# A GRU step with its gates reordered, its sigmoid halves folded into the blend, and its last channel block worked by batch element

## The chip, the cores and the metric

The kernel runs on one core of a Trainium2 chip. The metric is the device time of one execution in microseconds (us), the median over several executions. All runs compared here are of the undisturbed ("fast") state. The engines are called PE (matmuls), DVE (vector), ACT (activations) and POOL (GpSimd), as the profile calls them; the recorded texts also say TensorE, VectorE and ScalarE. An fp32 matmul or transpose of the source appears in the trace as two instructions, and counts below are of those.

## The reference

There are 64 graphs of 256 nodes with 256 channels. The first layer, a gated graph network, is nearly all of the work, and the change is in it:

```python
h = relu(layernorm(x))
for i in range(3):                                    # three steps
    m    = h @ weight[i]
    aggr = einsum('bst,bsd->btd', adj != 0, m)        # sums over neighbours
    gi, gh = aggr @ w_ih.T + b_ih, h @ w_hh.T + b_hh  # split into r, z, n
    r = sigmoid(i_r + h_r);  z = sigmoid(i_z + h_z)
    n = tanh(i_n + r * h_n)
    h = (1 - z) * n + z * h
x = x + h
# second layer: h = relu(layernorm(x)), graph attention with 4 heads, x = x + its output
```

## The kernel before

Two graphs make a pair (512 columns), and there are 32 pairs. A pair is a Python generator that emits its instructions stage by stage, and two pairs are interleaved, so that the attention part of the older pair lies beside the gates of the newer. When the program is built, a scheduler turns all this into one fixed list of instructions for each engine. As its lists show, it keeps roughly to the order of emission, but moves work forward that it takes to be ready.

The weights of the message are folded into those of the gates, so a step is: transpose h to rows and split it into hi and lo (`prows`), sum over neighbours (`pa`), then for each of two channel blocks the gates `hn, r, z, in` and the blend:

```python
for l in range(L):
    if l:
        rows_hi_lo(KD - 1, hT, hi, lo)          # rows of the last channel block (PE, then ACT and DVE)
    for e in range(KD):
        neighbours(e, aggr, hi, lo)             # sums of channel block e, both graphs
        yield                                   # a stage ends at each yield
    for c in range(KD):
        gate(p_hn, wT["hh"], g_n, hT, True, True)
        gate(p_r, wT["hh"], g_r, hT, True, False);  gate(p_r, w_in[:, l], g_r, aggr, False, True)
        gate(p_z, wT["hh"], g_z, hT, True, False);  gate(p_z, w_in[:, l], g_z, aggr, False, True)
        gate(p_in, w_in[:, l], g_n, aggr, True, True)
        # r = 0.5*tanh(./2)+0.5 (ACT, DVE); z likewise (ACT, POOL)
        # t = (p_hn + bh) * r; t = p_in + t (DVE); n = tanh(t + bi) (ACT)
        # d = h - n (POOL); d = z * d; hT2 = n + d (DVE)
        if c < KD - 1: yield
    ...                                         # rows of the first channel block of the next step
    yield
# transposes back (pback), x1 = x + h; yield; norm_relu_T(x1): second norm and its transposes (pt_b); yield
# val (pv); yield; attention: prow, softmax, ppT, po ...
STEPS = 1 + L * (2 + KD) + 3 + PB * (1 + KN)     # 22
# a new pair starts every STEPS // 2 + 1 = 12 stages
```

`hT` is the state with channels on the partitions, `aggr` the sums. Some names for later: a row join is the place between two steps where PE needs the rows of the last channel block (`prows`); a pair has two. The half-k matmuls of a gate are those that take the first channel block of h, which is ready a stage earlier. `pt_a` are the transposes after a pair's first norm; `zz`, `lk` and `nmx` belong to the softmax. A bank is one of the PSUM buffers into which PE writes; the program has four for the gates and four for the rest. Filler is work that stands in PE's list ahead of an instruction that waits.

Of the kernel before, what the change touches and what calls it, by code (L numbers as in the profile page):

```python
# [9 lines left out]
F32 = mybir.dt.float32  # L10
# [3 lines left out]
AF = mybir.ActivationFunctionType  # L14
ALU = mybir.AluOpType
AX = mybir.AxisListType

P = 128
# [4 lines left out]
EPS = 1e-5  # L23
# [3 lines left out]
def gated_gnn_then_gat_kernel(  # L27
# [25 lines left out]
    nc = tc.nc  # L53
    B, N, D = x.shape
    L = weight.shape[0]
# [3 lines left out]
    KD = D // P  # L59
# [14 lines left out]
    def bank(name):  # L74
        return ps_m.tile([P, 512], F32, tag="mm", name=name)
# [71 lines left out]

    w_nat = sb.tile([P, KD, D], F32, tag="d", name="w_nat")
# [36 lines left out]
    def norm_relu_T(src, name):  # L185

        st = small.tile([P, R, 6], F32, tag="st", name=f"st_{name}")
        mv = small.tile([P, R, 2], F32, tag="mv", name=f"mv_{name}")
        for r in range(R):
            nc.vector.bn_stats(st[:, r, :], src[:, r, :])  # L190
            nc.vector.bn_aggr(mv[:, r, :], st[:, r, :])
        rstd = small.tile([P, R], F32, tag="rstd", name=f"rstd_{name}")
        nc.vector.tensor_scalar_add(rstd, mv[:, :, 1], EPS)
        nc.gpsimd.tensor_tensor(rstd, rstd, mhalf, ALU.pow)
        xn = sb.tile([P, R, D], F32, tag="xn", name=f"xn_{name}")
        for r in range(R):
            nc.vector.tensor_scalar(
                xn[:, r, :], src[:, r, :], mv[:, r, 0:1], rstd[:, r : r + 1], op0=ALU.subtract, op1=ALU.mult
            )
        hT = sb.tile([P, KD, T], F32, tag="hT", name=f"hT_{name}", bufs=4)  # L200
        for k in range(KD):
            pt = bank(f"pt_{name}_{k}")
            for r in range(R):
                nc.tensor.transpose(pt[:, ts(r, P)], xn[:, r, ts(k, P)], ident)
            nc.scalar.activation(hT[:, k, :], pt, AF.Relu)
        return hT, xn

    def gate(pt, w, g, src, start, stop):
        for k in range(KD):
            nc.tensor.matmul(  # L210
                pt, w[:, k, ts(g, P)], src[:, k, :], start=start and k == 0, stop=stop and k == KD - 1
            )

    def pair(p):
# [6 lines left out]
        hT, xn = norm_relu_T(xt, f"a{p}")  # L221
# [7 lines left out]
        def rows_hi_lo(k, hT, hi, lo):  # L229

            pt = bank(f"prows_{hi.name}_{k}")
            for r in range(R):
                nc.tensor.transpose(pt[:, ts(r, P)], hT[:, k, ts(r, P)], ident)  # L233
            pt = pt.rearrange("q (r d) -> q r d", r=R)
            nc.scalar.copy(hi[:, :, ts(k, P)], pt)
            nc.vector.tensor_sub(lo[:, :, ts(k, P)], pt, hi.bitcast(F32)[:, :, ts(k, P)])

        def neighbours(e, aggr, hi, lo):
            pt = bank(f"pa_{aggr.name}_{e}")
            for i in range(PB):  # L240
                for s in range(KN):
                    for part in (hi, lo):
                        nc.tensor.matmul(  # L243
                            pt[:, ts(i, N)], part[:, i * KN + s, ts(e, P)], edge[:, i * KN + s, :],
                            start=(s == 0 and part is hi), stop=(s == KN - 1 and part is lo),
                        )
            nc.scalar.copy(aggr[:, e, :], pt)

        for l in range(L):
            n_ = f"{p}_{l}"  # L250
            aggr = sb.tile([P, KD, T], F32, tag="aggr", name=f"aggr_{n_}")
            if l:
                rows_hi_lo(KD - 1, hT, hi, lo)
            for e in range(KD):
                neighbours(e, aggr, hi, lo)
                yield
            hT2 = sb.tile([P, KD, T], F32, tag="hT", name=f"hT_{n_}", bufs=4)
            for c in range(KD):
# [7 lines left out]
                gate(p_r, w_in[:, l], g_r, aggr, False, True)  # L266
                gate(p_z, wT["hh"], g_z, hT, True, False)
                gate(p_z, w_in[:, l], g_z, aggr, False, True)
                gate(p_in, w_in[:, l], g_n, aggr, True, True)

                r_ = sb.tile([P, T], F32, tag="r", name=f"r_{n_}_{c}")
                nc.scalar.activation(r_, p_r, AF.Tanh, bias=brz[:, g_r : g_r + 1], scale=0.5)  # L272
                nc.vector.tensor_scalar(r_, r_, 0.5, 0.5, op0=ALU.mult, op1=ALU.add)  # L273
                z_ = sb.tile([P, T], F32, tag="z", name=f"z_{n_}_{c}")
                nc.scalar.activation(z_, p_z, AF.Tanh, bias=brz[:, g_z : g_z + 1], scale=0.5)  # L275
                nc.gpsimd.tensor_scalar(z_, z_, 0.5, 0.5, op0=ALU.mult, op1=ALU.add)  # L276
                t_ = sb.tile([P, T], F32, tag="t", name=f"t_{n_}_{c}")
                nc.vector.scalar_tensor_tensor(
                    t_, p_hn, bh[:, g_n : g_n + 1], r_, op0=ALU.add, op1=ALU.mult
                )  # L280
# [6 lines left out]
                nc.vector.tensor_mul(d_, z_, d_)  # L287
                nc.vector.tensor_add(hT2[:, c, :], n__, d_)  # L288
                if c < KD - 1:
                    yield  # L290
            if l < L - 1:
                if p == 0:
                    fold(l + 1)
                hi = sb.tile([P, R, D], F32R, tag="hi", name=f"hi_{p}_{l + 1}")
                lo = sb.tile([P, R, D], F32R, tag="lo", name=f"lo_{p}_{l + 1}")
                for k in range(KD - 1):
                    rows_hi_lo(k, hT2, hi, lo)
# [17 lines left out]
        hT, _ = norm_relu_T(x1, f"b{p}")  # L315
# [79 lines left out]
    STEPS = 1 + L * (2 + KD) + 3 + PB * (1 + KN)  # L395
# [41 lines left out]
```

## Time and profile before

| | before |
|---|---|
| time | 3027.39 us (3025.45 to 3027.95) |
| PE busy | 2891.5 of 3024.3 us, 96% |
| DVE, ACT, POOL busy | 58%, 32%, 17% |
| start of the first pair's `pback`, of the last pair's, end | 110.23, 2964.27, 3024.3 us |
| one pair in mid run | 92.07 us |

The best tool to find PE's gaps is the timeline of PE alone. Subtract from each distance between two starts what that instruction takes when nothing is in its way (a gate 0.429 us, `po` 0.1115, `pa` 0.1185, `pv` 0.223, a transpose 0.109); what is left over is lost. One stretch that the prediction does not show, in front of `pt_b`, looks like this (start, duration, engine, line, instruction, and in brackets how long PE was idle and for whom):

```profile
1495.30 0.88 PE L307 MATMUL pback<-ident,hT 128*128 128x128 f32 x6 [0.56 <-DVE hT L288]
1496.02 1.88 PE L210 MATMUL pr<-hT_a,hh_T 128*128 128x512 f32 x4
1497.73 1.02 PE L210 MATMUL pr<-aggr,w_in 128*128 128x512 f32 x2
1498.59 1.88 PE L210 MATMUL pz<-hT_a,hh_T 128*128 128x512 f32 x4
1501.17 0.67 PE L204 MATMUL pt_b<-ident,xn_b 128*128 128x128 f32 x4 [0.69 <-DVE xn_b L197]
```

Between the last `pback` and `pt_b` the list of PE holds 10 gate matmuls of the newer pair (10 x 0.429 = 4.29 us). The second norm takes longer than that, and 0.86 us are lost (the bracket says 0.69, because the modelled end of a matmul lies some 0.16 us after its slot).

### The profile page before, as it was taken

The numbers are of one execution on the slowest core, as the hardware profiler recorded it, in microseconds if no ns is written. First come the engines' busy times: TensorE is split into PE (matmuls) and PEld (weight loads), VectorE is DVE, ScalarE is ACT, GpSimd is POOL, SyncE is SP. The second block draws the span as 40 slices with busy tenths as digits, with TensorE's granted clock in tenths as the row PEclk, the third lists the DMA queues.
The fourth block names the chain that finished last, engine by engine and source line by source line (L and its number), as shares of the span: only waits on it lengthen the run. The fifth ranks groups of instructions, "written<-read, shape, count | busy, mean of one in ns | idle before, by whom it ended". The sixth has DMA issues, their size and how long they took to land.

```text
span 3024.3 us, 31009 instructions
## 1 busy us (share of the span) xinstructions
PE 2891.5 (96%) x11620; PEld 1689.6 (56%) x11620; DVE 1753.5 (58%) x3428; ACT 969.2 (32%) x2177; POOL 520.0 (17%) x583
## 2 busy tenths in 40 slices
PE   7999999999999999999999999999999999999996
PEld 4555555555555555555555555555555555555554
DVE  4555665555665555655556655556655566555554
ACT  1223332323333233333233323333332333233332
POOL 1111111111111111111111111111111111111111
PEclk9999999999999999999999999999999999999996
DMA  2000000000000000000000000000000000000000
GB/s 79 8 21 17 19 15 14 22 21 15 22 15 15 21 21 15 14 15 21 22 15 21 15 14 21 22 14 15 18 18 22 15 21 15 15 21 15 7 6 9
DMA packets 56085, 55.07 MB, mean 18 GB/s; under 512 B 4096, under 2 KB 55936, under 8 KB 55936
## 3 DMA queue, kind: packets, MB, share of 16 engines
q1 hardware_dynamic: 50688, 50.34, 5.3%
q10 hardware_dynamic: 5248, 2.76, 0.3%
q8 instruction: 92, 1.51, 0.2%
q14 instruction: 57, 0.47, 0.1%
HBM read 36.32 MB, written 16.78 MB: 18 GB/s over the span
## 4 chain that ended last, share of the span: by engine, by line
PE 71%; DVE 14%; POOL 6%; ACT 4%; issue 4%; DMA 0%; POOLq 0%; SPq 0%; DVEq 0%; ACTq 0%
PE pz L210 16%; PE pr L210 15%; PE pin L210 9%; PE po L382 7%; PE phn L210 7%; PE pa_aggr L243 5%; PE pv L321 4%; POOL d L286 4%; PE ppT L372 3%; DVE d L287 2%; DVE hT L288 2%; ACT pr L363 2%; DVE zz L346 2%; PE prows_hi L233 2%; ACT n L283 2%
## 5 line engine op out<-in xcount | busy, mean ns | idle before, releaser
L210 PE MATMUL pr<-aggr,w_in 128*128 128x512 f32 x768 | 366.0, 592 | 0.0
L210 PE MATMUL pin<-aggr,w_in 128*128 128x512 f32 x768 | 360.9, 592 | 0.0
L210 PE MATMUL pz<-aggr,w_in 128*128 128x512 f32 x768 | 360.9, 592 | 0.0
L272 ACT ACTIVATE r<-pr,brz 128x512 f32<-128x512 f32 x192 | 131.9, 687 | 685.3 <-PE pr L210 685.3
L276 POOL TENSOR_SCALAR z<-z 128x512 f32<-128x512 f32 x192 | 118.6, 618 | 1338.6 <-ACT z L275 1338.6
L281 DVE TENSOR_TENSOR t<-pin,t 128x512 f32<-128x512 f32 x192 | 132.5, 690 | 335.2 <-PE pin L210 334.6
L363 ACT ACTIVATE pr<-lk,nmx 128x256 f32<-128x256 f32 x512 | 254.5, 499 | 99.8 <-DVE nmx L359 99.5
L287 DVE TENSOR_TENSOR d<-z,d 128x512 f32<-128x512 f32 x192 | 148.6, 774 | 233.4 <-POOL d L286 233.4
L210 PE MATMUL phn<-hT,hh_T 128*128 128x512 f32 x512 | 256.4, 593 | 0.0
L382 PE MATMUL po<-val,prT 128*128 128x64 f32 x2048 | 250.2, 277 | 1.5 <-ACT prT L377 1.4
L210 PE MATMUL pr<-hT,hh_T 128*128 128x512 f32 x512 | 250.8, 593 | 0.0
L210 PE MATMUL pz<-hT,hh_T 128*128 128x512 f32 x512 | 250.8, 592 | 0.0
L210 PEld LDWEIGHTS pin<-aggr,w_in 128*128 128x128 f32 x768 | 146.2, 190 | 183.4 <-issue 183.4
L210 PEld LDWEIGHTS pz<-aggr,w_in 128*128 128x128 f32 x768 | 146.1, 190 | 183.5 <-issue 183.5
L382 PEld LDWEIGHTS po<-val,prT 128*128 128x128 f32 x2048 | 246.2, 196 | 3.3 <-ACT prT L377 3.1
L275 ACT ACTIVATE z<-pz,brz 128x512 f32<-128x512 f32 x192 | 131.3, 684 | 346.4 <-PE pz L210 346.4
L210 PEld LDWEIGHTS pr<-aggr,w_in 128*128 128x128 f32 x768 | 146.1, 190 | 170.7 <-issue 168.7
L273 DVE TENSOR_SCALAR r<-r 128x512 f32<-128x512 f32 x192 | 81.9, 426 | 259.6 <-ACT r L272 259.6
L346 DVE SCALAR_TENSOR_TENSOR zz<-prow,val,noedge 128x256 f32<-128x256 f32 x512 | 214.6, 476 | 1.4 <-PE prow L335 0.9
L243 PE MATMUL pa_aggr<-edge,hi 128*128 128x256 f32 x768 | 211.9, 307 | 1.0
L286 POOL TENSOR_TENSOR d<-hT,n 128x512 f32<-128x512 f32 x128 | 162.7, 1271 | 278.3 <-ACT n L283 278.3
L243 PE MATMUL pa_aggr<-edge,lo 128*128 128x256 f32 x768 | 194.8, 285 | 0.0
(91 smaller groups left out, 4164.9 us busy)
## 6 DMA issues: line engine op xcount, KB each, us to landing
x<-in_x_dram SPq DMA_DIRECT2D x32, 512.0 KB, 3.9
adj<-in_adj_dram SPq DMA_DIRECT2D x32, 512.0 KB, 3.9
out_dram<-o SPq DMA_DIRECT2D x32, 512.0 KB, 2.9
w_msg<-in_L_gnn_weight_dram ACTq DMA_DIRECT2D x1, 768.0 KB, 7.4
ih_nat<-in_L_gnn_w_ih_dram ACTq DMA_DIRECT2D x1, 768.0 KB, 11.4
hh_nat<-in_L_gnn_w_hh_dram ACTq DMA_DIRECT2D x1, 768.0 KB, 15.3
w_nat<-in_L_gnn_W_dram ACTq DMA_DIRECT2D x1, 256.0 KB, 8.3
a_exp<-in_L_gnn_a_dram ACTq DMA_DIRECT2D x8, 0.2 KB, 2.3
```

The source lines that it names most:

```text
L210: nc.tensor.matmul(pt, w[:, k, ts(g, P)], src[:, k, :], start=start and k == 0, stop=stop and k == KD - 1)
L243: nc.tensor.matmul(pt[:, ts(i, N)], part[:, i * KN + s, ts(e, P)], edge[:, i * KN + s, :], start=(s == 0 and part is hi), stop=(s == KN - ...
L272: nc.scalar.activation(r_, p_r, AF.Tanh, bias=brz[:, g_r : g_r + 1], scale=0.5)
L275: nc.scalar.activation(z_, p_z, AF.Tanh, bias=brz[:, g_z : g_z + 1], scale=0.5)
L276: nc.gpsimd.tensor_scalar(z_, z_, 0.5, 0.5, op0=ALU.mult, op1=ALU.add)
L281: nc.vector.tensor_add(t_, p_in, t_)
L286: nc.gpsimd.tensor_sub(d_, hT[:, c, :], n__)
L287: nc.vector.tensor_mul(d_, z_, d_)
L321: nc.tensor.matmul(pt[:, :VW], hT[:, k, ts(r, P)], w_val[:, k, :], start=(k == 0), stop=(k == KD - 1))
L346: nc.vector.scalar_tensor_tensor(zz[:, h, :], rowp[h // 2][:, ts(h % 2, N)], val[:, r, D + h : D + h + 1], noedge[:, r, :], op0=ALU.add, o ...
L363: nc.scalar.activation(pr[:, h, :], lk[:, h, :], AF.Exp, bias=nmx[:, h : h + 1], accum_out=den[:, h : h + 1])
L382: nc.tensor.matmul(po[:, ts(h, C)], prT[:, j, h, :], val[:, i * KN + j, ts(h, C)], start=(j == 0), stop=(j == KN - 1),)
```

## The change

Its intent is to shorten the chain between the last gate of a step and the next work of PE. (1) The gate order becomes `hn, r, in, z`, so that n and h - n are made while z's matmuls run. (2) The halves of sigmoid(x) = 0.5 tanh(x/2) + 0.5 are folded into the products, which saves two instructions and needs one more on ACT (`hn`). (3) The last channel block of a step, its rows, the sums and the second norm go by batch element. (4) As sums by element need no stage between them, a step has one stage fewer: 19 stages, and pairs start 10 apart; before it was 22 and 12.

```diff
-    def norm_relu_T(src, name):                          # cut: whole norm and transposes
+    def norm(src, name, parts=1):                        # cut: statistics, pow and scaling in parts
+    def relu_T(xn, name, parts=1):
+        for i in range(parts):
+            for k in range(KD):
+                pt = bank(f"pt_{name}_{i}_{k}")
...
-        def neighbours(e, aggr, hi, lo):                 # one channel block, both elements
+        def neighbours(i, aggr, hi, lo):                 # one element, both channel blocks
...
-            for e in range(KD):
-                neighbours(e, aggr, hi, lo)
-                yield
+            for i in range(PB):
+                neighbours(i, aggr, hi, lo)
+            yield
...
                 gate(p_r, w_in[:, l], g_r, aggr, False, True)
+                gate(p_in, w_in[:, l], g_n, aggr, True, True)
                 gate(p_z, wT["hh"], g_z, hT, True, False)
                 gate(p_z, w_in[:, l], g_z, aggr, False, True)
-                gate(p_in, w_in[:, l], g_n, aggr, True, True)
...
+                nc.scalar.activation(hn, p_hn, AF.Identity, bias=bhh[:, c : c + 1], scale=0.5)
                 nc.scalar.activation(r_, p_r, AF.Tanh, bias=brz[:, g_r : g_r + 1], scale=0.5)
-                nc.vector.tensor_scalar(r_, r_, 0.5, 0.5, op0=ALU.mult, op1=ALU.add)
-                nc.scalar.activation(z_, p_z, AF.Tanh, bias=brz[:, g_z : g_z + 1], scale=0.5)
-                nc.gpsimd.tensor_scalar(z_, z_, 0.5, 0.5, op0=ALU.mult, op1=ALU.add)
-                nc.vector.scalar_tensor_tensor(t_, p_hn, bh[:, g_n : g_n + 1], r_, op0=ALU.add, op1=ALU.mult)
+                nc.vector.scalar_tensor_tensor(t_, r_, 1.0, hn, op0=ALU.add, op1=ALU.mult)
...
                 nc.gpsimd.tensor_sub(d_, hT[:, c, :], n__)
-                nc.vector.tensor_mul(d_, z_, d_)
-                nc.vector.tensor_add(hT2[:, c, :], n__, d_)
+                parts = PB if c == KD - 1 else 1
+                for i in range(parts):
+                    at_ = ts(i, T // parts)
+                    nc.scalar.activation(z_[:, at_], p_z[:, at_], AF.Tanh, bias=..., scale=0.5)
+                    nc.vector.scalar_tensor_tensor(z_[:, at_], z_[:, at_], 1.0, d_[:, at_], op0=ALU.add, op1=ALU.mult)
+                    nc.vector.scalar_tensor_tensor(hT2[:, c, at_], z_[:, at_], 0.5, n__[:, at_], op0=ALU.mult, op1=ALU.add)
...
-        hT, _ = norm_relu_T(x1, f"b{p}")
+        hT = relu_T(norm(x1, f"b{p}", PB), f"b{p}", PB)
...
-    STEPS = 1 + L * (2 + KD) + 3 + PB * (1 + KN)
+    STEPS = 1 + L * (1 + KD) + 3 + PB * (1 + KN)
```

The buffer of the normalized rows, `xn`, also goes from two to one.

More of the change, by code (lines that the diff above doesn't have):

```diff
@@ L146, in gated_gnn_then_gat_kernel @@
     nc.vector.tensor_scalar_mul(brz, brz, 0.5)
+    bhh = const.tile([P, KD], F32, name="bhh")
+    nc.vector.tensor_scalar_mul(bhh, bh[:, 2 * KD :], 0.5)
     w_nat = sb.tile([P, KD, D], F32, tag="d", name="w_nat")
@@ L182, in gated_gnn_then_gat_kernel @@
     nc.vector.tensor_copy(b_val[:, D:], pb[:, : 2 * H])
-    def norm_relu_T(src, name):
-        st = small.tile([P, R, 6], F32, tag="st", name=f"st_{name}")
-        mv = small.tile([P, R, 2], F32, tag="mv", name=f"mv_{name}")
-        for r in range(R):
-            nc.vector.bn_stats(st[:, r, :], src[:, r, :])
-            nc.vector.bn_aggr(mv[:, r, :], st[:, r, :])
-        rstd = small.tile([P, R], F32, tag="rstd", name=f"rstd_{name}")
-        nc.vector.tensor_scalar_add(rstd, mv[:, :, 1], EPS)
-        nc.gpsimd.tensor_tensor(rstd, rstd, mhalf, ALU.pow)
-        xn = sb.tile([P, R, D], F32, tag="xn", name=f"xn_{name}")
-        for r in range(R):
-            nc.vector.tensor_scalar(
-                xn[:, r, :], src[:, r, :], mv[:, r, 0:1], rstd[:, r : r + 1], op0=ALU.subtract, op1=ALU.mult
-            )
-        hT = sb.tile([P, KD, T], F32, tag="hT", name=f"hT_{name}", bufs=4)
-        for k in range(KD):
-            pt = bank(f"pt_{name}_{k}")
-            for r in range(R):
-                nc.tensor.transpose(pt[:, ts(r, P)], xn[:, r, ts(k, P)], ident)
-            nc.scalar.activation(hT[:, k, :], pt, AF.Relu)
-        return hT, xn
+    def norm(src, name, parts=1):
+        xn = sb.tile([P, R, D], F32, tag="xn", name=f"xn_{name}", bufs=1)
+        for i in range(parts):
+            n_ = R // parts
+            rows = range(i * n_, (i + 1) * n_)
+            st = small.tile([P, n_, 6], F32, tag="st", name=f"st_{name}_{i}")
+            mv = small.tile([P, n_, 2], F32, tag="mv", name=f"mv_{name}_{i}")
+            for j, r in enumerate(rows):
+                nc.vector.bn_stats(st[:, j, :], src[:, r, :])
+                nc.vector.bn_aggr(mv[:, j, :], st[:, j, :])
+            rstd = small.tile([P, n_], F32, tag="rstd", name=f"rstd_{name}_{i}")
+            nc.vector.tensor_scalar_add(rstd, mv[:, :, 1], EPS)
+            nc.gpsimd.tensor_tensor(rstd, rstd, mhalf[:, :n_], ALU.pow)
+            for j, r in enumerate(rows):
+                nc.vector.tensor_scalar(
+                    xn[:, r, :], src[:, r, :], mv[:, j, 0:1], rstd[:, j : j + 1], op0=ALU.subtract, op1=ALU.mult
+                )
+        return xn
@@ L208, in gate @@
+    def relu_T(xn, name, parts=1):
+        hT = sb.tile([P, KD, T], F32, tag="hT", name=f"hT_{name}", bufs=4)
+        n_ = R // parts
+        for i in range(parts):
+            for k in range(KD):
+                pt = bank(f"pt_{name}_{i}_{k}")
+                for j in range(n_):
+                    nc.tensor.transpose(pt[:, ts(j, P)], xn[:, i * n_ + j, ts(k, P)], ident)
+                nc.scalar.activation(hT[:, k, ts(i, n_ * P)], pt[:, : n_ * P], AF.Relu)
+        return hT
     def gate(pt, w, g, src, start, stop):
@@ L220, in pair @@
         nc.vector.tensor_scalar(noedge, at, 1.0, MASKED, op0=ALU.not_equal, op1=ALU.mult)
-        hT, xn = norm_relu_T(xt, f"a{p}")
+        xn = norm(xt, f"a{p}")
+        hT = relu_T(xn, f"a{p}")
         hi = sb.tile([P, R, D], F32R, tag="hi", name=f"hi_{p}_0")
@@ L227, in pair, with rows_hi_lo @@
         yield
-        def rows_hi_lo(k, hT, hi, lo):
-            pt = bank(f"prows_{hi.name}_{k}")
-            for r in range(R):
-                nc.tensor.transpose(pt[:, ts(r, P)], hT[:, k, ts(r, P)], ident)
-            pt = pt.rearrange("q (r d) -> q r d", r=R)
-            nc.scalar.copy(hi[:, :, ts(k, P)], pt)
-            nc.vector.tensor_sub(lo[:, :, ts(k, P)], pt, hi.bitcast(F32)[:, :, ts(k, P)])
-        def neighbours(e, aggr, hi, lo):
-            pt = bank(f"pa_{aggr.name}_{e}")
-            for i in range(PB):
+        def rows_hi_lo(k, hT, hi, lo, parts):
+            n_ = R // parts
+            for i in range(parts):
+                rows = slice(i * n_, (i + 1) * n_)
+                pt = bank(f"prows_{hi.name}_{k}_{i}")
+                for j in range(n_):
+                    nc.tensor.transpose(pt[:, ts(j, P)], hT[:, k, ts(i * n_ + j, P)], ident)
+                pt = pt[:, : n_ * P].rearrange("q (r d) -> q r d", r=n_)
+                nc.scalar.copy(hi[:, rows, ts(k, P)], pt)
+                nc.vector.tensor_sub(lo[:, rows, ts(k, P)], pt, hi.bitcast(F32)[:, rows, ts(k, P)])
+        def neighbours(i, aggr, hi, lo):
+            pt = bank(f"pa_{aggr.name}_{i}")
+            for e in range(KD):
                 for s in range(KN):
@@ L243, in neighbours @@
                         nc.tensor.matmul(
-                            pt[:, ts(i, N)], part[:, i * KN + s, ts(e, P)], edge[:, i * KN + s, :],
+                            pt[:, ts(e, N)], part[:, i * KN + s, ts(e, P)], edge[:, i * KN + s, :],
                             start=(s == 0 and part is hi), stop=(s == KN - 1 and part is lo),
                         )
-            nc.scalar.copy(aggr[:, e, :], pt)
+            nc.scalar.copy(aggr[:, :, ts(i, N)], pt.rearrange("q (e t) -> q e t", e=KD))
         for l in range(L):
@@ L252, in pair @@
             if l:
-                rows_hi_lo(KD - 1, hT, hi, lo)
-            for e in range(KD):
-                neighbours(e, aggr, hi, lo)
-                yield
+                rows_hi_lo(KD - 1, hT, hi, lo, PB)
+            for i in range(PB):
+                neighbours(i, aggr, hi, lo)
+            yield
             hT2 = sb.tile([P, KD, T], F32, tag="hT", name=f"hT_{n_}", bufs=4)
@@ L266, in pair @@
                 gate(p_r, w_in[:, l], g_r, aggr, False, True)
+                gate(p_in, w_in[:, l], g_n, aggr, True, True)
                 gate(p_z, wT["hh"], g_z, hT, True, False)
                 gate(p_z, w_in[:, l], g_z, aggr, False, True)
-                gate(p_in, w_in[:, l], g_n, aggr, True, True)
+                hn = sb.tile([P, T], F32, tag="hn", name=f"hn_{n_}_{c}")
+                nc.scalar.activation(hn, p_hn, AF.Identity, bias=bhh[:, c : c + 1], scale=0.5)
                 r_ = sb.tile([P, T], F32, tag="r", name=f"r_{n_}_{c}")
                 nc.scalar.activation(r_, p_r, AF.Tanh, bias=brz[:, g_r : g_r + 1], scale=0.5)
-                nc.vector.tensor_scalar(r_, r_, 0.5, 0.5, op0=ALU.mult, op1=ALU.add)
-                z_ = sb.tile([P, T], F32, tag="z", name=f"z_{n_}_{c}")
-                nc.scalar.activation(z_, p_z, AF.Tanh, bias=brz[:, g_z : g_z + 1], scale=0.5)
-                nc.gpsimd.tensor_scalar(z_, z_, 0.5, 0.5, op0=ALU.mult, op1=ALU.add)
                 t_ = sb.tile([P, T], F32, tag="t", name=f"t_{n_}_{c}")
-                nc.vector.scalar_tensor_tensor(
-                    t_, p_hn, bh[:, g_n : g_n + 1], r_, op0=ALU.add, op1=ALU.mult
-                )
+                nc.vector.scalar_tensor_tensor(t_, r_, 1.0, hn, op0=ALU.add, op1=ALU.mult)
                 nc.vector.tensor_add(t_, p_in, t_)
@@ L286, in pair @@
                 nc.gpsimd.tensor_sub(d_, hT[:, c, :], n__)
-                nc.vector.tensor_mul(d_, z_, d_)
-                nc.vector.tensor_add(hT2[:, c, :], n__, d_)
+                z_ = sb.tile([P, T], F32, tag="z", name=f"z_{n_}_{c}")
+                parts = PB if c == KD - 1 else 1
+                for i in range(parts):
+                    at_ = ts(i, T // parts)
+                    nc.scalar.activation(z_[:, at_], p_z[:, at_], AF.Tanh, bias=brz[:, g_z : g_z + 1], scale=0.5)
+                    nc.vector.scalar_tensor_tensor(z_[:, at_], z_[:, at_], 1.0, d_[:, at_], op0=ALU.add, op1=ALU.mult)
+                    nc.vector.scalar_tensor_tensor(
+                        hT2[:, c, at_], z_[:, at_], 0.5, n__[:, at_], op0=ALU.mult, op1=ALU.add
+                    )
                 if c < KD - 1:
@@ L296, in pair @@
                 for k in range(KD - 1):
-                    rows_hi_lo(k, hT2, hi, lo)
+                    rows_hi_lo(k, hT2, hi, lo, 1)
             hT = hT2
```

## The prediction

> **What bounds the kernel now.** I read the page's busy table first. It shows TensorE (PE) busy for nearly the whole span, and no other engine above 58%:
>
> ```profile
> PE 2891.5 (96%) x11620; PEld 1689.6 (56%) x11620; DVE 1753.5 (58%) x3428; ACT 969.2 (32%) x2177; POOL 520.0 (17%) x583
> PEclk9999999999999999999999999999999999999996
> ```
>
> So the change, which leaves every matmul and transpose in place, can win at most what PE loses to waiting: 3024.3 - 2891.5 = 133 us of idle, plus stalls that a modelled matmul end hides. Next I looked at the waits of PE alone over the whole run:
>
> ```profile
> PE prows_hi L233 <- DVE hT L288: 50.7, 31, 1.6
> PE pt_b L204 <- DVE xn_b L197: 26.1, 32, 4.3
> PE pback L307 <- DVE hT L288: 21.7, 32, 4.2
> PE pw_ih L113 <- DMA ih_nat<-in_L_gnn_w_ih_dram: 12.8, 1, 12.8
> PE ppT L372 <- ACT pr L363: 10.9, 2, 5.8
> ```
>
> The columns are total, number and longest. Three waits come once per pair (32 pairs; the first comes 31 times because it needs a neighbouring pair): the row transposes after a step's last channel block, the transposes back after the last step, and the transposes after the second norm. The two others are the start and the tail.
>
> Then the timeline gives the period. The transposes back of the first and of the last pair start at
>
> ```profile
> 110.23 0.38 PE L307 MATMUL pback<-ident,hT 128*128 128x128 f32 x2
> ...
> 2964.27 0.38 PE L307 MATMUL pback<-ident,hT 128*128 128x128 f32 x2
> ```
>
> which is 2854.04 us for 31 pairs, 92.07 us each. What lies outside is 110 us of start and 60 us of tail.
>
> How much of 92.07 is real streaming? Start-to-start distances in the undisturbed stretches: 24 gate matmuls from 1511.97 to 1522.27, 0.429 us each; 16 po in 1.735 (0.108); 8 pa in 0.95 (0.119); 8 transposes in 0.87 (0.109); 16 pv in 3.70 (0.231). A pair has 144 gate matmuls (61.8 us), 64 po (6.9), 48 pa (5.7), 16 pv (3.7) and 88 transposes (9.6): 87.7 us. So 4.3 us per pair are lost. In the timeline of one pair I find them: 1.80 before prows_hi, 0.86 before pt_b, 0.72 before pback, together 3.4 us; the other 0.9 us is a dozen gaps of 0.1 to 0.2 us. The largest one, on PE:
>
> ```profile
> 1520.56 1.88 PE L210 MATMUL pin<-aggr,w_in 128*128 128x512 f32 x4
> 1522.27 0.60 PE L233 MATMUL prows_hi<-ident,hT 128*128 128x128 f32 x4
> 1522.71 1.04 PE L372 MATMUL ppT<-ident,pr 128*128 128x128 f32 x8
> 1523.58 1.02 PE L210 MATMUL phn<-hT,hh_T 128*128 128x512 f32 x2
> 1524.44 1.02 PE L210 MATMUL pr<-hT,hh_T 128*128 128x512 f32 x2
> 1525.30 1.02 PE L210 MATMUL pz<-hT,hh_T 128*128 128x512 f32 x2
> 1527.96 0.63 PE L233 MATMUL prows_hi<-ident,hT 128*128 128x128 f32 x4 [1.64 <-DVE hT L288]
> ```
>
> and what ran meanwhile on the other engines:
>
> ```profile
> 1523.06 0.69 DVE L281 TENSOR_TENSOR t<-pin,t 128x512 f32<-128x512 f32 x1
> ...
> 1524.29 0.72 ACT L283 ACTIVATE n<-t,bi 128x512 f32<-128x512 f32 x1
> ...
> 1525.09 1.27 POOL L286 TENSOR_TENSOR d<-hT_a,n 128x512 f32<-128x512 f32 x1 [2.00 <-ACT n L283]
> ...
> 1526.39 0.69 DVE L287 TENSOR_TENSOR d<-z,d 128x512 f32<-128x512 f32 x1 [0.69 <-POOL d L286]
> ...
> 1527.12 0.69 DVE L288 TENSOR_TENSOR hT<-n,d 128x512 f32<-128x512 f32 x1
> ```
>
> The reader is to see five dependent instructions on three engines between the last gate (stream done at 1522.27) and the transposes at 1527.96: 5.69 us, against 3.89 us of other PE work. Undisturbed (t at 1480.42 to the blend's end at 1484.79) this chain takes 4.4 us.
>
> **What the Trainium skill says.** "ScalarE: Activation LUTs", section "What ACT_TABLE_LOAD costs", puts an activation with a bias pointer at about 280 ns + 0.833 ns an element: 706 ns at 512, 493 at 256. The trace agrees: r takes 687 ns, and the exps, 256 wide with a bias pointer, 499. Its section on table sets has exp and tanh in one set and identity in all; the trace has one table load in the whole run, so the new Identity should add none. "VectorE: DVE Perf Modes", section "Mode 2×_2P", says an fp32 op with one tensor source in SBUF gets two results a cycle and a two-tensor op one; the trace has 426 ns for the r scaling against 690 for the adds, so the DVE instruction removed is a cheap one. "TensorE: Matmul & The Clock Gate", Part 1, says that idling over a window of about 3.4 us halves the clock; here the clock falls to 0.50 only in the tail, after two idle stretches of 4.25 and 4.28 us.
>
> **The change part by part.**
> *Folding.* Removes 192 DVE scalings (426 ns, 82 us) and 192 POOL scalings (618 ns, 119 us); adds 192 Identity activations, which I cost as r (687 ns, 132 us). Splits add about 40 us of fixed cost on ACT and 40 on DVE. ACT goes to about 1150 us (39%), DVE to about 1700, POOL to 400. None bounds, so none of this counts by itself; it is off PE's path.
> *Gate order.* The in gate is followed by 8 z matmuls, 3.43 us. t, n and d (0.69 + 0.72 + 1.27 and some 0.4 of handover, 3.1 us) fit beside them. After the last matmul remain the z tanh and two DVE instructions.
> *By batch element.* Half widths: tanh 0.49 (the exp's row), each DVE op 0.425 (the 128x256 rows), handovers as in the trace (0.26 after a matmul, 0.1 otherwise): 0.26 + 0.49 + 0.1 + 0.43 + 0.1 + 0.43 + 0.1 = 1.9 us to the first half, about 2.75 to the second. The filling work at the join is at least 0.44 (first rows) + 2.58 (half-k gates) = 3.0 us. The wait before prows_hi should vanish (1.80), and so should that before pback (0.72), which has pt_a and pa beside it.
> *Second norm by halves.* From pback to pt_b now 5.87 us (1495.30 to 1501.17). For one half: 0.6 to the add, 0.69, two rows of statistics 1.0, 0.25, pow 1.1, scaling 0.5, 0.15: 4.3, or 5.0 with the other half's add ahead. It starts 2 to 3 us sooner too. The compiler orders PE's work by its own estimates, though, and put pt_b too early before; I leave 0.4 of the 0.86.
> *Schedule.* A step has 3 stages for 4, so pairs start 10 of 19 stages apart (12 of 22 before). At both row joins the neighbour's exps will now be near; before, only at one.
>
> Sum per pair: 1.80 + 0.72 + 0.46 = 2.98, less 0.2 for new short gaps at the extra splits: 2.8 us, 31 x 2.8 = 87 us. The start barely changes (82.8 us for pair 0 alone, of which about 82 streams). In the tail the 4.25 wait loses some 2.5, the norm about 1, a warmer clock about 1: 4.5. Total 91: 3027.4 - 91 = 2936 us.
>
> **The rivals.** *All waits vanish:* 31 x 3.4 + 5 = 110, 2917 us. For it: plenty of ready gate work at every join. Against: the short gaps come from handovers that remain. *ScalarE becomes the wait:* from 1519.74 to 1525.9 it is nearly without pause, mostly exps (0.5 us plus 0.18 for the sum). z's two tanh pieces, hi's copies and now hn queue there in order. If each loses one or two exps, about 1 us stays at both joins and pt_b keeps its wait: gain 1.2 a pair, 2985 us. Against: the new chain has 1.1 us of slack at the join. *The new offset lacks filler* or the half-banks of pt_b and prows crowd the four PSUM buffers: a new wait of 2 to 3 us a pair, 3020 to 3060. For it: four pt_b tiles where there were two. Against: the number of ready gates is unchanged. *A wait on xn's single buffer:* the second norm must wait for the next pair's pt_a; those come right at the join already, so I expect little.
>
> **Range and chances.** 2% is 60.5 us, 1.8 us a pair with the tail. Two of the three waits closing gives that; only the ScalarE rival or the bad offset misses it. Range 2908 to 2985. Faster 0.80, same 0.16, slower 0.04.
>
> **What would show it.** PE busy near 98%; no PE wait on hT of tens of us in total; a period between pbacks near 89.3 us; POOL's idle no longer ending on z; DVE and ACT near the totals above. Wrong if the period stays above 91 us, if prows_hi or pa waits for ACT hi, or if the clock leaves 1.00 in mid run.

## The result, and the profile after

The changed kernel takes 3050.82 us (3050.58 to 3051.02) against 3027.67 us in the same rounds: a ratio of 1.0078, 95% interval 1.0061 to 1.0095. So it is 0.8% slower, within 2% of before, where a gain of 3% was predicted. A ratio here is the mean time of one kernel's fast runs over that of the other's of the same rounds, so it is not quite the ratio of the medians quoted.

The busy row of the page of the changed kernel:

```profile
PE 2908.6 (95%) x11620; PEld 1708.2 (56%) x11620; DVE 1645.3 (54%) x3525; ACT 1129.3 (37%) x2593; POOL 437.5 (14%) x423
```

PE has the same 11620 instructions. DVE and POOL lost and ACT gained about what was expected, but PE's idle time grew from 133 to 140 us. The waits of PE over the whole run (total, number, longest) say where; the names `ows_hi` and `rows_hi` are `prows_hi` under clipped names:

```profile
PE pt_b L216 <- DVE xn_b L203: 74.9, 64, 3.9
...
PE phn L222 <- ACT hT_a L217: 10.0, 31, 0.3
PE ows_hi L249 <- DVE hT L307: 9.2, 30, 0.5
PE prows_hi L249 <- DVE hT L307: 9.1, 31, 0.4
...
PE pback L328 <- DVE hT L307: 1.5, 1, 1.5
```

The waits for `hT`, which were 72 us (`prows_hi` and `pback`), are down to 20. But `pt_b` now waits twice per pair, 74.9 us instead of 26.1.

The span splits into start, 31 periods and tail at the first `pback` of the first and the last pair, which are at 109.95 and 2991.21 us now. Start: 0.28 us shorter. Tail: 57.6 us instead of 60.05, so 2.5 us shorter, less than the 4.5 predicted but of the right sign. The 31 periods take 2881.3 us instead of 2854.0, and they are where the loss lies (27.22 - 0.28 - 2.46 = 24.48 us, the difference of the spans, 3048.80 - 3024.32). Of the periods, 23 take 92.6 us, seven 94.1, and one 92.9; before, all but the last took 92.07 to 92.10.

By the subtraction explained above, the lost time of one pair at whole clock lies here:

| place, us lost per pair | before | predicted | after |
|---|---|---|---|
| `pt_b`, transposes after the second norm | 0.86 | 0.40 | 1.47 + 1.12 |
| first row join: `prows_hi`, and the sums behind it | 1.80 | 0 | 0.35 + 0.36 |
| second row join | 0.14 | 0.14 | 0.56 |
| `pback` | 0.73 | 0 | 0 |
| first work on the next pair's state beside `pback` | 0.29 | 0.29 | 0.59 |
| the rest | 0.46 | 0.66 | 0.32 |
| sum | 4.28 | 1.49 | 4.77 |

The column "predicted" is spread out from the prediction's terms: its 0.9 us of short gaps and its 0.2 for new ones are put at the second join (0.14), beside `pback` (0.29) and in the rest (0.66). Its rival "new offset lacks filler" named 3020 to 3060 us.

Here is the stretch in front of `pt_b` in the changed kernel, on PE, without the sums that lie between its last pieces:

```profile
1507.42 0.82 PE L328 MATMUL pback<-ident,hT 128*128 128x128 f32 x6
1508.07 1.02 PE L222 MATMUL phn<-hT_a,hh_T 128*128 128x512 f32 x2
1508.93 1.88 PE L222 MATMUL pr<-hT_a,hh_T 128*128 128x512 f32 x4
1512.13 0.67 PE L216 MATMUL pt_b<-ident,xn_b 128*128 128x128 f32 x4 [1.31 <-DVE xn_b L203]
1513.75 0.41 PE L216 MATMUL pt_b<-ident,xn_b 128*128 128x128 f32 x2 [0.96 <-DVE xn_b L203]
...
1514.12 0.39 PE L216 MATMUL pt_b<-ident,xn_b 128*128 128x128 f32 x2
```

From `pback` to the first `pt_b` 4.71 us pass; the prediction's estimate for a half was 4.3 to 5.0. So the norm by halves is 1.16 us faster, as worked out. What the prediction did not see is the row between: only 6 gate matmuls (2.58 us) stand there, where there were 10 (4.29 us). Right behind the first pieces of `pt_b` come the 16 sums of the next pair, then `pv`, and then the gates with `aggr`. The sums need nothing that is missing (in e5 below, 13 of them run ahead of `pt_b`). PE works its list in order, so it stands in front of `pt_b` with work in hand.

Seven pairs lose another 1.53 us. The table of windows shows why (window, its length, busy time and instructions of PE, PEld, DVE, ACT, POOL, then PE's granted clock). The first two lines are a long and an ordinary pair, the next two the 9 us around `pt_b` in each:

```profile
1410.74:1504.88 94.14, 90.85 (x362) 53.56 (x361) 50.99 (x109) 35.23 (x81) 13.67 (x13) 0.98 0.05 17
1504.88:1597.46 92.58, 89.30 (x362) 52.17 (x361) 50.90 (x109) 35.23 (x81) 13.66 (x13) 1.00 0.06 18
1418.00:1427.00 9.00, 8.04 (x40) 7.14 (x41) 5.17 (x19) 2.49 (x6) 1.71 (x2) 0.81 0.03 9
1512.00:1521.00 9.00, 7.92 (x44) 6.44 (x45) 5.65 (x20) 2.49 (x6) 1.71 (x2) 1.00 0.06 19
```

The trace's record of the clock has seven stretches at 0.50 in mid run, each 3.41 us long and each beginning just after the waits at `pt_b` (0.5 x 3.41 / 9 = 0.19 off the mean of that window). The kernel before has none until its tail. These stretches are worth 7 x 1.53 = 10.7 us of the 27.2; the rest, 16.5 us, is 0.53 us a pair. Why seven pairs and not the others can be worked out: laid out from the recorded starts in windows of 3.413 us, and filled with the slots of the subtraction, PE is busy for 0.28 to 0.36 of the window that precedes each of the seven stretches; every other mid-run window holds at least 0.38.

The third reading is the first row join. All engines, without weight loads and the instructions that do not matter here:

```profile
1535.53 1.22 DVE L380 TENSOR_REDUCE nmx<-lk 128x4 f32<-128x1024 f32 x1
1536.02 1.88 PE L222 MATMUL pz<-aggr,w_in 128*128 128x512 f32 x4
1536.66 0.69 DVE L295 TENSOR_TENSOR t<-pin,t 128x512 f32<-128x512 f32 x1
...
1537.79 0.71 ACT L297 ACTIVATE n<-t,bi 128x512 f32<-128x512 f32 x1
...
1538.40 0.81 ACT L305 ACTIVATE z<-pz,brz 128x256 f32<-128x256 f32 x2
1538.57 1.27 POOL L300 TENSOR_TENSOR d<-hT_a,n 128x512 f32<-128x512 f32 x1 [12.40 <-ACT n L297]
...
1539.88 0.76 DVE L306 SCALAR_TENSOR_TENSOR z<-z,d 128x256 f32<-128x256 f32 x2 [2.44 <-POOL d L300]
...
1541.12 0.75 PE L249 MATMUL prows_hi<-ident,hT 128*128 128x128 f32 x4 [0.19 <-DVE hT L307]
```

The in gate's matmuls had their slots until 1534.31 (four from 1532.59), but t starts at 1536.66, 2.35 us later, because DVE is working through the older pair's softmax (`lk`, `nmx`, 1.2 us each). The exps on ACT add a little: n starts 0.44 us after t's end, 0.09 in e6, where the queue is empty. So d ends at 1539.84, 2.1 us after z's last matmul (slot until 1537.74), and the blend waits for d and not for z, whose tanh is done by 1539.21. The chain behind the last gate is 3.38 us instead of the 1.9 predicted. The gate order has less filler ready, too: the half-k part of z, which stood before `prows_hi` in the old order, is gone, and 3.03 us are left of 3.89 (the first row transposes, `ppT` and four gate matmuls). 3.38 - 3.03 is the 0.35 us lost in front of `prows_hi`.

### The profile page after: what moved, and what is told of

Same layout as the page of the kernel before. It is cut to its first block, busy times and chain, and to the rows that moved or that the text cites. A ratio compares the mean times of both kernels' runs of the same rounds, so it can differ in the third digit from the quotient of the medians.

```text
span 3048.8 us, 31482 instructions
## 1 busy us (share of the span) xinstructions
PE 2908.6 (95%) x11620; PEld 1708.2 (56%) x11620; DVE 1645.3 (54%) x3525; ACT 1129.3 (37%) x2593; POOL 437.5 (14%) x423
## 4 chain that ended last, share of the span: by engine, by line
PE 58%; DVE 19%; issue 13%; POOL 5%; ACT 4%; DMA 0%; POOLq 0%; ACTq 0%; SPq 0%; DVEq 0%
PE pr L222 12%; PE pz L222 11%; PE po L403 7%; PE pin L222 7%; PE pa_aggr L260 7%; PE phn L222 5%; PE pv L342 4%; POOL d L300 4%; DVE zz L367 4%; DVE nmx L380 3%; DVE lk L373 3%; PE ppT L393 2%; DVE hT L307 2%; DVE z L306 2%; POOL rstd_b L201 1%
## 5 line engine op out<-in xcount | busy, mean ns | idle before, releaser
L306 DVE SCALAR_TENSOR_TENSOR z<-z,d 128x256 f32<-128x256 f32 (+1 forms) x288 | 139.2, 511 | 470.8 <-ACT z L305 334.6
L294 DVE SCALAR_TENSOR_TENSOR t<-r,hn 128x512 f32<-128x512 f32 x192 | 132.7, 691 | 461.7 <-ACT r L292 461.7
L290 ACT ACTIVATE hn<-phn,bhh 128x512 f32<-128x512 f32 x192 | 131.9, 687 | 364.7 <-PE phn L222 363.1
L222 PE MATMUL pz<-hT,hh_T 128*128 128x512 f32 x512 | 240.6, 593 | 0.0
L305 ACT ACTIVATE z<-pz,brz 128x256 f32<-128x256 f32 (+1 forms) x288 | 145.6, 539 | 252.2 <-PE pz L222 249.3
L297 ACT ACTIVATE n<-t,bi 128x512 f32<-128x512 f32 x192 | 137.5, 716 | 228.8 <-DVE t L295 228.8
L412 POOL TENSOR_TENSOR o<-o,x 128x256 f32<-128x256 f32 x128 | 116.2, 908 | 640.2 <-DVE o L407 607.5
```

The source lines that it names most:

```text
L222: nc.tensor.matmul(pt, w[:, k, ts(g, P)], src[:, k, :], start=start and k == 0, stop=stop and k == KD - 1)
L290: nc.scalar.activation(hn, p_hn, AF.Identity, bias=bhh[:, c : c + 1], scale=0.5)
L294: nc.vector.scalar_tensor_tensor(t_, r_, 1.0, hn, op0=ALU.add, op1=ALU.mult)
L297: nc.scalar.activation(n__, t_, AF.Tanh, bias=bi[:, g_n : g_n + 1])
L305: nc.scalar.activation(z_[:, at_], p_z[:, at_], AF.Tanh, bias=brz[:, g_z : g_z + 1], scale=0.5)
L306: nc.vector.scalar_tensor_tensor(z_[:, at_], z_[:, at_], 1.0, d_[:, at_], op0=ALU.add, op1=ALU.mult)
```

## The experiments

Theory: the new gate order and the folding pay; what takes the gain away is the order of PE's list, above all that `pt_b` now stands in front of the next pair's sums. That came with the merged stage and the new offset: the sums of the newer pair used to be emitted partly in the stage of `pback`, and are now emitted after the second norm. Rivals: the halves themselves cost (more instructions, more handovers, four PSUM banks for `pt_b` where there were two); ACT's extra work costs; the gate order does not help.

In each experiment the lists of PE can be read in the built program before it runs. What stands between the last `pback` and `pt_b`, and what came of it:

| kernel | between `pback` and `pt_b` | us | lost at `pt_b` | period, us |
|---|---|---|---|---|
| before | 4 `pr`, 2 `pr` with `aggr`, 4 `pz` | 4.29 | 0.86 | 92.07 |
| changed | 2 `phn`, 4 `pr` | 2.58 | 1.47 + 1.12 | 92.6, some 94.1 |
| e2 | 2 `phn`, 4 `pr` | 2.58 | 2.57 | 92.5, some 94.0 |
| e5 | 13 sums, 4 `phn`, 2 `pr` | 4.11 | 0 + 1.01 | 91.07 |
| e4 | 5 sums, 4 `phn`, 4 `pr` | 4.02 | 0.12 + 1.01 | 90.63 |
| e1 | 4 `phn`, 4 `pr`, 2 `pr` with `aggr` | 4.29 | 0.86 | 90.61 |
| e7 | the same and 5 sums | 4.88 | 0.27 + 0.54 | 90.04 |
| e10 | 4 `pr` and 16 others of a block | 8.58 | 0 | 87.68 |

### e1: fold and gate order alone

```diff
 (against the changed kernel)
+ neighbours(e, ...) with a yield after each;  STEPS with L * (2 + KD)    # as before
-                parts = PB if c == KD - 1 else 1
+                parts = 1
-                rows_hi_lo(KD - 1, hT, hi, lo, PB)
+                rows_hi_lo(KD - 1, hT, hi, lo, 1)
-        hT = relu_T(norm(x1, f"b{p}", PB), f"b{p}", PB)
+        hT = relu_T(norm(x1, f"b{p}"), f"b{p}")
```

It keeps the single `xn` buffer.

> The new gate order and the folded sigmoids alone: full widths, sums by channel block, two stages for the sums and the old offset of 12 of 22, second norm whole. Theory (order: PE waits where the compiler's fixed order puts a transpose ahead of work that is ready): in PE's order pt_b again has 4.3 us of gates between pback and it, so its wait is near the 0.9 us a pair of before; prows_hi has 3.0 us of filler against a chain of 3.5 us or a little more, so it waits 0.5 to 0.8; pback has only 1 us of sums against a chain of 2.6, so it waits 1.4. Sum about as before: period 91.5 to 92.3 us, 3010 to 3035 us. Rival (the folding and ScalarE's extra work cost the time): near the changed kernel, 3045 to 3055 us.

Measured: 2979.26 us, ratio 0.9841 (0.9826 to 0.9855), period 90.61 us. It is better than either expectation. `pt_b` loses the 0.86 us foretold and `prows_hi` 1.16, but `pback` nothing: the next pair's 8 transposes `pt_a` stand ahead of it as well, which I had not counted. So parts (1) and (2) of the change win 1.6%, and ACT's extra work (37% busy in all) does not stand in the way. All of the loss is in parts (3) and (4).

### e2: the second norm whole

```diff
-        hT = relu_T(norm(x1, f"b{p}", PB), f"b{p}", PB)
+        hT = relu_T(norm(x1, f"b{p}"), f"b{p}")
```

> The changed kernel with its second norm and pt_b whole again. Theory (order): PE's order still has only two thirds of phn and pr, 2.6 us, between pback and pt_b, because the sums of the next pair still come after pt_b; the chain from pback to pt_b is 5.9 us whole, so pt_b waits about 2.5 us in one piece instead of 1.5 + 1.1, the period stays at 92.3 to 92.8 us, the half-clock stretches stay, 3040 to 3055 us. Rival (the halves and their four PSUM banks cause it): pt_b waits 0.9 as before, the period falls to 90.8, no half-clock stretches, 2990 to 3000 us.

Measured: 3045.36 us, ratio 1.0062 (1.0045 to 1.0078). The wait is there in one piece instead of two:

```profile
PE pt_b L216 <- DVE xn_b L203: 78.8, 32, 4.6
```

The half-clock stretches stay too, six in mid run. With two PSUM banks and whole width `pt_b` loses 2.57 us, so neither the halves of the norm nor their banks are the cause (e4 clears the other halves). The same 2.58 us of work stand ahead of it.

### e5: the transposes emitted one stage later

```diff
-        hT = relu_T(norm(x1, f"b{p}", PB), f"b{p}", PB)
+        xn = norm(x1, f"b{p}", PB)
         yield
+        hT = relu_T(xn, f"b{p}", PB)
         val = ...
```

> The changed kernel with pt_b emitted one stage later, in front of val: same instructions, and PE's order now has the next pair's 16 sums, phn and half of pr (4.1 us) between pback and pt_b. Theory (order): pt_b waits 0 to 1.0 us a pair instead of 2.6, the 0.5 us before phn goes too, no half-clock stretch in mid run; period 90.0 to 91.0 us, 2960 to 2990 us. Rival (halves and their banks, or the extra ScalarE work): 3035 to 3055 us.

Measured: 2992.35 us, ratio 0.9885 (0.9871 to 0.99), period 91.07 us, a little above what I had written.

```profile
PE pt_b L216 <- DVE xn_b L203: 30.5, 33, 3.9
```

The same instructions, emitted in another order, are 58 us faster than the changed kernel: the first half of `pt_b` waits no more, the second 1.0 us, and there is no half-clock stretch in mid run. What I had wrong is the small loss beside `pback`: the 0.5 us stayed, now in front of the sums instead of `phn`.

### e6: the newer pair first

```diff
 (e5, and)
-        for g in list(live):
+        for g in list(live)[::-1]:
```

> As e5, and in every stage the newer pair's instructions are emitted ahead of the older pair's, so that the gate chain goes ahead of the older pair's softmax in DVE's and ScalarE's queues too, and pt_b has a whole channel block of gates (10 us) ahead of it. Theory (order): pt_b's wait is 0; t starts within 0.3 us of the in gate instead of 2.3 us after it at the row join, so the chain from the last z matmul to the first row transpose is about 2 to 2.6 us instead of 3.5; period 88.8 to 90.3 us, 2925 to 2970 us. Rival (the split work itself and its handovers cost it, whatever the order): 3030 us or more. What could spoil it: the older pair's softmax is starved and po or ppT starts to wait.

Measured: 3061.73 us, ratio 1.0115 (1.01 to 1.013), period 93.37 us. My number is refuted, though both steps happen: `pt_b` loses nothing, and at the first row join the first transposes start 2.17 us after z's last matmul (1539.98 to 1542.15; 1.9 were predicted for an empty queue). What I had named as the spoiler takes more than that back:

```profile
PE pa_aggr L260 <- DVE zz L368: 42.5, 61, 1.1
PE pr L222 <- ACT aggr L264: 41.8, 62, 0.7
PE pa_aggr L260 <- DVE lo L252: 32.3, 62, 0.5
```

The softmax that was pushed back is in DVE's list behind the blend, but ahead of `lo`. It also holds the PSUM banks that the sums need (`zz` reads `prow` out of them). 116.6 us of new waits are more than was won. To put one chain first everywhere is no cure.

### e4: two stages for the sums again

```diff
             for i in range(PB):
                 neighbours(i, aggr, hi, lo)
-            yield
+                yield
-    STEPS = 1 + L * (1 + KD) + 3 + PB * (1 + KN)
+    STEPS = 1 + L * (2 + KD) + 3 + PB * (1 + KN)
```

All halves stay; only part (4) is undone.

> The changed kernel, with all its halves, but the sums of the two batch elements in two stages again, so that pairs start 12 of 22 stages apart as before. Theory (the emission order around pt_b costs the time, not the halves): PE's order has 5 of the first 8 sums, phn and pr (4.0 us) between pback and pt_b, so the first half of pt_b waits 0 to 0.5 us, the second half some 1.0 as in e5; no half-clock stretches; period 90.8 to 91.6 us, 2970 to 2995 us. Rival (the halves of z, rows and sums cost it): near the changed kernel's 92.6 us without the half clock, 3035 us or more.

Measured: 2978.96 us, ratio 0.9841 (0.9827 to 0.9856), period 90.63 us. The wait at `pt_b` is less than half of the changed kernel's 74.9:

```profile
PE pt_b L216 <- DVE xn_b L203: 30.6, 33, 3.9
```

So part (4) alone, the merged stage with its offset, makes the difference between 0.8% slower and 1.6% faster. Against e1, which differs in the halves, it is neither better nor worse: they win at the first row join (0.73 lost instead of 1.16) what they lose at `pt_b` (1.13 instead of 0.86) and beside `pback` (0.59 instead of 0.44).

### e7: halves of z only

```diff
 (e1, and)
-                parts = 1
+                parts = PB if c == KD - 1 else 1
```

> e1 with the one split that shortens the chain at the joins: z's tanh and blend of the last channel block by batch element; rows, sums and second norm whole. Expected: prows_hi, which needs both halves, gains little or nothing (1.2 us in e1, 0.9 to 1.3 here), because two half instructions take longer than one whole; PE's order has 4.9 us instead of 4.3 us between pback and pt_b, so pt_b waits 0.3 instead of 0.9; period 89.9 to 90.5 us, 2955 to 2975 us. Rival (any z split costs through ScalarE's and DVE's queues): above 90.8 us, 2985 us or more.

Measured: 2961.51 us, ratio 0.9782 (0.9767 to 0.9796), period 90.04 us. The time is as expected, but not for my reason: at the first join `prows_hi` loses 0.36 us, not 0.9 to 1.3. The halves do shorten the chain, because ACT works on the second half of z while DVE blends the first. `pt_b` loses 0.27 + 0.54 in pieces, as its transposes come as fast as DVE scales rows.

### e9: the folding with the old gate order

```diff
 (e1, and)
                 gate(p_r, w_in[:, l], g_r, aggr, False, True)
-                gate(p_in, w_in[:, l], g_n, aggr, True, True)
                 gate(p_z, wT["hh"], g_z, hT, True, False)
                 gate(p_z, w_in[:, l], g_z, aggr, False, True)
+                gate(p_in, w_in[:, l], g_n, aggr, True, True)
```

> e1 with the gates in the old order (hn, r, z, in): the folding alone. If the gate order made e1's gain, the chain after the last gate is t, n, d and two blends again, 4.4 us or more, prows_hi waits about 1.5 to 1.8 and pback about 0.7, period 91.5 to 92.1 us, 3010 to 3030 us. Rival (the folding made it, by emptying DVE and POOL): near e1, 90.6 us, 2980 us.

Measured: 3102.48 us, ratio 1.0236 (1.0192 to 1.028), and with more spread than any other kernel (3077.9 to 3111.1 us). Neither number fits. As long as the clock is whole the period is 92.33 us, close to the theory's range: 0.71 lost at `pback`, 0.86 at `pt_b`, 2.05 at the first join. The gate order, then, makes e1's gain (92.33 to 90.61), and the folding alone makes none (before: 92.07). The new order without the folding was not run. The rest is the clock. From 1072 us on nearly every pair has a stretch of 6.83 us at half clock, soon after that one wait of 2.05 us, and takes 95.5 us. Most stretches begin 95.57 us apart, which is 28 x 3.413: the longer period puts the next wait at the same place in its window, so it is hit again (worked out from the starts, not tested). A mid-run pair and an early one, by windows:

```profile
2000.00:2092.00 92.00, 88.83 (x341) 52.05 (x340) 48.98 (x93) 32.62 (x71) 11.48 (x11) 0.96 0.06 18
700.00:792.00 92.00, 89.15 (x360) 51.91 (x360) 50.99 (x101) 34.19 (x74) 12.51 (x12) 1.00 0.06 18
```

### e10: e1 with pairs 10 of 22 stages apart

```diff
-        if nxt < NPAIR and tick % (STEPS // 2 + 1) == 0:
+        if nxt < NPAIR and tick % (STEPS // 2 - 1) == 0:
```

> e1 with pairs started 10 of 22 stages apart instead of 12 (three pairs are alive for a while). PE's order then has a whole channel block of gates (10.3 us) between pback and pt_b, and val's or po's matmuls between the two row transposes of a join. Theory (PE waits only where its order lacks work ahead of a transpose): pt_b waits 0, prows_hi 0 to 0.5; period 88.6 to 89.8 us, 2915 to 2955 us. Rival (more overlap starves the older pair's softmax or the PSUM buffers, as in e6 where the sums waited for zz): new waits of pa, pr or ppT, 2980 us or more.

Measured: 2888.09 us, ratio 0.9542 (0.9526 to 0.9558), period 87.61 us on average. This beats both kernels by far, and it is below the 2915 to 2955 us that I had expected: the rival is refuted, and my own number was too cautious. PE is busy 99%, and the waits over the whole run are those of start and tail (each once or twice):

```profile
PE 2846.6 (99%) x11620; PEld 1701.5 (59%) x11620; DVE 1662.3 (58%) x3237; ACT 1091.7 (38%) x2369; POOL 424.0 (15%) x391
```

```profile
PE pw_ih L113 <- DMA ih_nat<-in_L_gnn_w_ih_dram: 12.8, 1, 12.8
PE ppT L392 <- ACT pr L383: 10.9, 2, 5.8
PE pt_b L216 <- DVE xn_b L203: 4.6, 1, 4.6
PE pback L327 <- DVE hT L306: 2.1, 1, 2.1
```

The period is what the prediction worked out as pure streaming, 87.7 us. At the join the z chain still takes 2.9 us behind the last matmul (1450.40 to 1453.28), but 16 `pv` (3.6 us) stand in front of the transposes that need it.

### e11: the kernel before with the same offset

The same edit on the kernel before.

> The kernel before with its pairs started 10 of 22 stages apart instead of 12, nothing else. It tells what of e10's gain is the offset alone. PE's order now has 8 us of gates between pback and pt_b (wait 0), and val's 16 matmuls (3.6 us) or po and prow between the two row transposes of a join; but the old chain (in gate last: t, n, d, two blends, 4.4 us or more) still stands behind pback, with 2.6 us of gates in front of it. Theory (the offset closes the waits that have filler, the gate order the rest): 1.5 to 3 us a pair stay lost, mostly at pback and one join; period 89.5 to 91 us, 2940 to 2985 us. Rival 1 (the offset alone does it): period 88 us or less, under 2905 us. Rival 2 (the offset only pays with the new gate order): 91.5 us or more, 3005 us or more.

Measured: 2985.47 us, ratio 0.9866 (0.9849 to 0.9882), period 90.75 us. The time just misses its range; what is left over lies where it was expected, and at one place more:

```profile
PE ppT L372 <- ACT pr L363: 28.9, 33, 5.8
PE pback L307 <- DVE hT L288: 27.0, 32, 4.2
PE prows_hi L233 <- DVE hT L288: 23.3, 31, 0.8
```

The offset alone is worth 1.3%, fold and gate order alone 1.6%, both together 4.6%.

### e12 and e13: the changed kernel with other offsets

The same line with `STEPS // 2` (9 of 19 stages) and `STEPS // 2 - 1` (8 of 19).

> The changed kernel with 9 of 19 stages instead of 10. Its PE order is nearly that of e6 (prow of the older pair between the row transposes, both channel sums behind it). If the order on PE is what decides, its waits are those of e6 too: sums waiting for zz to free a PSUM bank and for lo, gates for aggr, together about 4 us a pair beyond streaming; pt_b, with only phn in front of its first half, waits 1 to 2 us more: period 92 to 94.5 us, 3025 to 3090 us. Rival (starting pairs closer together helps in itself): under 2985 us.

> The changed kernel, all of its halves kept, with 8 of 19 stages instead of 10. PE's order has a whole channel block of gates and po (12 us) between pback and pt_b, val's matmuls or po and ppT between the row transposes of a join. Theory (the halves cost little; the order did): nothing waits for more than 0.3 us; period 87.6 to 88.8 us, 2885 to 2920 us. Rival (the halves cost short stalls wherever they are): 0.26 + 0.1 + 0.4 us at each join and the gap between pt_b's halves stay, period 89 us or more, 2930 us or more.

Measured: e12 3087.09 us, ratio 1.0201 (1.0186 to 1.0216), period 94.17 us, with the waits of e6 nearly to the digit (42.8, 41.9 and 32.2 us). Only `pt_b`'s part is smaller than I had it, 0.7 us a pair. e13 2890.02 us, ratio 0.9547 (0.9533 to 0.9561), period 87.70 us on average. All halves are in e13, and a pair in mid run takes 87.83 us, 0.14 more than in e10. So the halves cost next to nothing, and with work ahead of the transposes they are not needed either: e10 without them is as fast. From 8 to 9 to 10 of 19 stages the time goes 2890, 3087, 3051 us with the same instructions.

## Why the prediction was wrong

Predicted were 2936 us (2908 to 2985), with 0.80 for faster; measured were 3050.8.

- **What bounds the kernel** was right, and so was the sum of streaming: e10 and e13 reach the 87.7 us a pair.
- **The folding's cost off PE's path** was right: ACT 1129 us (about 1150 predicted), DVE 1645 (1700), POOL 438 (400). `hn` took 687 ns as costed, a half z 465 ns against the estimate of 493 from the Trainium skill ("ScalarE: Activation LUTs", section "What ACT_TABLE_LOAD costs"), the half blends 420 ns against 425. e9 shows that it earns nothing by itself.
- **The gate order** was right in kind. e1 less e9 is 1.7 us a pair at whole clock, and e6 shows the short chain, 2.17 us. The step "t, n and d fit beside z's matmuls" failed at the first row join: t came 2.35 us late behind the neighbour's softmax on DVE, and of the term "1.80 vanishes" 0.35 stayed in front of `prows_hi`. The prediction had placed the rival in ACT's queue; it was mostly DVE's. Its 3.0 us of filler at the join came true by luck: it counted six half-k gates, but there are four and eight `ppT`, which it had left out.
- **"Less 0.2 for new short gaps"** was mis-sized. With sums by element the first sum needs the last rows at once, so the first join got 0.36 us behind the transposes; the second join went from 0.14 to 0.56. With 0.30 more beside `pback` that is 1.08 us.
- **The step that failed** is "second norm by halves ... I leave 0.4 of the 0.86". The chain was sized well (4.71 us measured, 4.3 to 5.0 predicted). But the prediction did not count the filler ahead of `pt_b`. Its 0.4 fits only the 4.3 us of the old trace, and against the rival of missing filler it wrote "the number of ready gates is unchanged". The merged stage with its offset moved the next pair's sums behind `pt_b`, and the filler went from 10 gate matmuls to 6, 2.58 us. The term was to become 0.40 and became 2.59. In all, 0.73 (`pback`) + 1.45 (first join) - 1.73 (`pt_b`) - 1.08 (new gaps) + 0.14 (the rest) = -0.49 us a pair, where +2.8 was predicted. e2 (halves undone: still 2.57), e5 (emission undone: 1.01) and e4 (stages undone: 1.13) show that it is the order. "For it: plenty of ready gate work at every join" was true and no help: ready work behind a waiting instruction does not count.
- **The clock** was not in the sum. I had expected it to leave 1.00 in the tail only, and had named a mid-run drop as a sign of being wrong. The concentrated waits cost another 10.7 us by half-clock stretches. The prediction also misread the old tail: its wait of 4.28 us lies inside the first half-clock stretch (2968.39 to 2978.63), and the second one, from 2985.45, begins in the 5.8 us that `ppT` waits for the last softmax.
- **Two smaller slips.** "Two of the three waits closing gives that" does not hold for `pback` and `pt_b`, 0.72 + 0.86 = 1.58 us, under the 1.8 needed. The rival of `xn`'s single buffer did not come true: e10 and e13 keep that buffer and stream.

In the end the rival "new offset lacks filler", with its 3020 to 3060 us, was right, and 0.04 for all that is slower, together with 0.16 for within 2%, gave it too little. Its other half, PSUM banks crowded by the half-banks, is not what happened: e2 keeps the wait with two banks at `pt_b`, and e13 streams with all half-banks. What stays open is by which estimates the scheduler puts `pt_b` where it does; only its lists were seen.

## What to carry to other kernels

When a queue is worked in order, a chain and the work ahead of its end belong together: when a change moves stages or offsets, count anew what stands in the list before each instruction that waits, and do not take the filler from the old trace. Read the built list: what was expected from it held for e2, e4, e12 and e13, and for e10 it was too cautious. Try the offset between interleaved streams as a parameter of its own after every such change: here 8, 9 and 10 of 19 stages differ by 7%, more than all the instruction work of the change.

## What the Trainium skill lacked or had wrong

- "TensorE: Matmul & The Clock Gate", Part 1: its table has the half clock come after at least one idle window of about 3.4 us (further on it tells of shorter pauses that do so, without a length). Here it came after one wait of 2.05 us (e9), one of 2.57 (e2), or 1.47 + 1.12 within 4 us (changed). Worked out as above, the windows before the 33 mid-run stretches of these three kernels were not idle but filled to 0.19 to 0.39; among all other mid-run windows of the 13 traces only five are filled as little (0.35 to 0.39). The emptiest holds 0.44 in the kernel before, with its single wait of 1.80 us, and 0.45 in e6, which loses 5.4 us a pair in pieces of up to 1.25; neither has a stretch.
- The same part calls the window free-running, and the trace agrees: the mid-run stretches last 3.41 or 6.83 us, and in the changed kernel they begin 372.05 or 464.2 us apart, 109 and 136 times 3.413. It speaks of the phase for the warm-up at a kernel's start only. In mid run, too, it depends on the phase whether a wait is punished: the same wait cost nothing in 24 of 31 pairs and 1.53 us in seven.
